# A row of exponentials per head, written to memory once per partition and read with shifted rows, in place of sixteen decay tiles, in a lightning-attention kernel

## The chip, the cores and the metric

The kernel runs on one core of a Trainium2 chip. The metric is the device time of one execution in microseconds (us); several executions are timed and the median counts. One more execution is taken with the hardware profiler, and every view of the profile comes from that one. Engines are named as in the profile: PE is TensorE's matmul, PEld its weight load, DVE is VectorE, ACT is ScalarE, POOL is GpSimd, SP is SyncE. SPq is SP's sequencer, which here issues nearly all DMAs.

## The reference, cut to what matters

The input x holds 4 sequences of 512 tokens with 512 features. It is normalised, goes through a linear attention with a decay per head, and is gated by a router.

```python
xn = layernorm(x)
qkv = silu(xn @ w_qkv.T)            # 16 heads of 128: q, k, v
# per head, slope s, blocks of BLK tokens, arr = 1 .. BLK
idx = arr[:, None] - arr[None, :]
diag_decay = where(idx >= 0, exp(-s * idx), 0)
o = (q * exp(-s * arr)) @ kv + ((q @ k.T) * diag_decay) @ v
kv = exp(-s * BLK) * kv + (k * exp(-s * (BLK - arr))).T @ v
o = norm_w * o * rsqrt(mean(o * o) + 1e-6) * sigmoid(xn @ w_gate.T)
s = o @ w_out.T
scores = softmax(xn @ router_w.T + router_b)      # 64 experts, the 8 largest count
g = silu(xn * sum(top8) + top8 @ expert_bias)
out = x + s * g
```

All is float32. The kernel uses blocks of 128 tokens in place of 64, which is the same sum cut elsewhere. What matters here is `diag_decay` with the decay of q: for one head both are made of the values exp(-s * d) for distances d from 0 to 128, and of zeros.

## The kernel before, in words

Every projection is a float32 product made of three passes over a hi and a lo part (`PASSES`): hi is a cast to the fast matmul type by ACT (`split_hi`, L100), lo is what is left, by DVE or POOL (`split_lo`, L103). A `unit` (matmuls at L496) computes a 2 x 2 block product with seven products in place of eight, from sums of blocks (S1 to S4 of the weights, T1 to T4 of the tokens); a `plain_unit` (L528) takes the eight products. The results of a unit are combined by DVE adds at L487, each of which reads the PSUM bank of a product.

The work runs in three stages. The **v stage** (0 to about 200 us) loads x in tiles of 128 tokens of two sequences, normalises them (`layer_norms`, `normalise_x` L204), transposes them on PE (`transpose`, pt at L253, copied to xf by ACT at L254), splits them into blocks (B11, T1, B21, B22 and the sums), computes the router's logits (lg, L314) and makes v in 16 units k = 0 to 15, eight for each half of the heads (`n1` is 8). The first two units are plain ones, while the sums of the weights are being made. `ws[0]` holds the weights of the first half, `ws[1]` those of the second. v goes to memory: the tiles `vo` come from a pool tagged `vout` with four buffers, one unit fills all four, and each is stored by a DMA at L582. The **head stage** (about 200 to 880 us) makes q, k and the gate per head and runs the attention. The **output stage** (880 us to the end) multiplies with w_out (po, L797).

The order of the work is written out by hand. A unit takes lists `after[0]` to `after[6]`, one for each of its products, with steps to be issued on all engines behind that product; the loop `for k, (p, t) in enumerate(tiles + again)` fills them. Each engine runs its own instructions in that order. DMAs of SP run on one queue in the order of issue, with eight completion semaphores taken in turn: a DMA waits for the one eight places before it. Four small loads at the start (slopes, rw, rb, nw, L878 to L881) are issued by ACT.

The decay tiles: `make_dist` writes two 128 x 128 tables of distances (POOL), `make_decays` takes 16 Exps of 128 x 256 on ACT (L168), `mask_decays` clears one triangle of each with an affine_select on POOL (L172) and stores each tile of 128 KB to memory (L177). In the head stage `load_decay` (L651) reads one tile per head and pair of sequences, 32 in all; the first 128 columns multiply the scores (`at`), the other 128 multiply q (`qd`). The Exps and selects run in three groups (7, 5 and 4 heads) among the first tile's work:

```python
make_decays(ds, hs[0])
prep[0]["stats"]()
prep[0]["norms"]()
ws[0].split_one("A11", nc.vector, hi=True)
prep[0]["turn"]()
load_pair(stage, *tiles[2])
mask_decays(ds, hs[0])
```

In the second half of the v stage, `load_xf` (L300) reads back xf of a tile (xf_again), from which POOL makes the blocks once more (`combine`); it is issued by SP in `after[0]` of the units k = 8 to 11.

Of the kernel before, what the change touches and what calls it, by code (L numbers as in the profile page):

```python
# [8 lines left out]
F32 = mybir.dt.float32  # L9
F32R = mybir.dt.float32r  # L10
AF = mybir.ActivationFunctionType
ALU = mybir.AluOpType
# [38 lines left out]
def kernel(  # L51
# [47 lines left out]
    def split_hi(hi, src):  # L99
        nc.scalar.copy(hi, src)  # L100
# [12 lines left out]
    dist = const.tile([P, 2, P], F32, tag="dist", name="dist")  # L113
    rest_of = const.tile([P, 1], F32, tag="rest_of", name="rest_of")
    kdecay = const.tile([P, NH], F32, tag="kdecay", name="kdecay")
    bdecay = const.tile([P, NH], F32, tag="bdecay", name="bdecay")

    decay_d = [dram.tile([P, 2, P], F32, tag=f"decay{h}", name=f"decay_{h}") for h in range(NH)]  # L120
    v_d = {
        (b, g): dram.tile([NT, P, VW], F32, tag=f"v{b}_{g}", name=f"v_{b}_{g}")
        for b in range(B) for g in range(NH // VH)
# [19 lines left out]
    def warm_up(n):  # L143
        ps = ps_o.tile([P, P], F32, tag="o", name="warm")
        for _ in range(n):
            nc.tensor.transpose(ps, ident, ident)

    def make_dist():  # L150
        nc.gpsimd.iota(
            dist[:, 0, :], pattern=[[-1, P]], base=0, channel_multiplier=1,
            allow_small_or_imprecise_dtypes=True,
        )
        nc.gpsimd.iota(
            dist[:, 1, :], pattern=[[-1, P]], base=-1, channel_multiplier=0,
            allow_small_or_imprecise_dtypes=True,
        )
# [4 lines left out]
        nc.gpsimd.tensor_scalar(dist[:, 0, :], dist[:, 0, :], 0.0, None, ALU.min)  # L163


    def make_decays(d, hs):
        for h in hs:
            nc.scalar.activation(d[h // 4][:, h % 4], dist, AF.Exp, scale=slopes[:, h : h + 1])  # L168

    def mask_decays(d, hs):  # L170
        for h in hs:
            nc.gpsimd.affine_select(  # L172
                d[h // 4][:, h % 4, 0], d[h // 4][:, h % 4, 0], pattern=[[1, P]],
                compare_op=ALU.is_ge, fill=0.0, base=0, channel_multiplier=-1,
            )
        for h in hs:
            nc.sync.dma_start(out=decay_d[h], in_=d[h // 4][:, h % 4])  # L177


    stats = [const.tile([P, NT, 2], F32, tag=f"stats{b}", name=f"stats{b}") for b in range(B)]  # L180
# [63 lines left out]
    xfs = {}  # L244


    def transpose(stage, p, j, t):
        b = p * PB + j
        if j == 0:
            xfs[p, t] = stage.tile([P, PB, FC, P], F32, tag="xf", name=f"xf_{p}_{t}", bufs=2)  # L250
        pt = ps_sc.tile([P, FC, P], F32, tag="sc", name=f"pt_{b}_{t}")
        for c in range(FC):
            nc.tensor.transpose(pt[:, c, :], xts[b, t][:, bass.ts(c, P)], ident)  # L253
        nc.scalar.copy(xfs[p, t][:, j], pt)  # L254

    def halves(xf):
        return xf[:, 0, 0:KC], xf[:, 1, 0:KC], xf[:, 0, KC:], xf[:, 1, KC:]
# [47 lines left out]
            nc.sync.dma_start(out=blocks_d[n][:, t], in_=blocks[p, n].bitcast(F32)[:, t])  # L305


    def logits(stage, p, t):
        if t == 0:
            scores[p] = stage.tile([P, PB, NT, E], F32, tag="scores", name=f"scores_{p}", bufs=2)  # L310
        ps = ps_sc.tile([P, PB, E], F32, tag="sc", name=f"lg_{p}_{t}")
        for j in range(PB):
            for c in range(FC):
                nc.tensor.matmul(  # L314
                    ps[:, j], xfs[p, t][:, j, c, :], rw[:, c, :], start=(c == 0), stop=(c == FC - 1)
                )
        nc.vector.tensor_tensor(
            scores[p][:, :, t, :], ps, rb[:, None, :].to_broadcast([P, PB, E]), ALU.add
        )
# [328 lines left out]

    def load_decay(p, h, attp):
        dec[p, h] = attp.tile([P, 2, P], F32, tag="dec", name=f"dec_{p}_{h}", bufs=3)  # L650
        nc.sync.dma_start(out=dec[p, h], in_=decay_d[h])  # L651


    def chunks(a):
# [198 lines left out]
    def load_pair(stage, p, t):  # L853
        for j in range(PB):
            load_x(stage, p * PB + j, t)
# [19 lines left out]
    make_first()  # L875

    nc.scalar.activation(kdecay[:, 0:NT], mhalf, AF.Exp)
    nc.scalar.dma_start(out=slopes, in_=slope.to_broadcast([P, NH]))  # L878
    nc.scalar.dma_start(out=rw, in_=router_w)
    nc.scalar.dma_start(out=rb, in_=router_b.to_broadcast([P, E]))  # L880
    nc.scalar.dma_start(out=nw, in_=norm_w)  # L881
    make_dist()
    warm_up(WARM)
# [5 lines left out]
    nc.scalar.activation(kdecay, slopes, AF.Exp, scale=rest_of[:, 0:1])  # L889
    nc.scalar.activation(bdecay, slopes, AF.Exp, scale=-float(P))  # L890
    ds = [
        sump.tile([P, KC * VW], F32, tag=f"sum{i}", name=f"mkdecay_{i}").rearrange(
            "p (h a m) -> p h a m", a=2, m=P
        ) for i in range(4)
    ]
    hs = range(0, 7), range(7, 12), range(12, NH)
    make_decays(ds, hs[0])
    prep[0]["stats"]()
    prep[0]["norms"]()
    ws[0].split_one("A11", nc.vector, hi=True)  # L900
    prep[0]["turn"]()
    load_pair(stage, *tiles[2])
    mask_decays(ds, hs[0])
    warm_up(6)
    prep[0]["sums"]()
    ws[0].split_one("A12", nc.gpsimd, 0)
    ws[0].split_one("A12", nc.vector, 1)
    prep[0]["logits"]()
    prep[1]["stats"]()
    ws[0].split_one("A21", nc.vector)  # L910
    make_decays(ds, hs[1])
    prep[1]["norms"]()
    load_pair(stage, *tiles[3])
    mask_decays(ds, hs[1])
    ws[0].split_one("A22", nc.gpsimd)
    make_decays(ds, hs[2])
    mask_decays(ds, hs[2])

    for k, (p, t) in enumerate(tiles + again):
        g, after = k // n1, nothing()  # L920
        for unit_of, what in ((n1 - 3, (0, "top")), (n1 - 2, (0, "less")), (n1 + 2, (1, "top")), (n1 + 3, (1, "less"))):
            if k == unit_of:
                after[2].append(lambda what=what: scores_less(*what))
        if n1 - NT <= k < n1:
            after[6].append(lambda p=p, t=t: keep_blocks(p, t))
        if k + 1 < n1:
            after[0 if k else 1].append(prep[k + 1]["turn"])
            if 0 < k < n1 - 3:
                after[0].append(lambda k=k: load_pair(stage, *tiles[k + 3]))
            after[1].append(prep[k + 1]["sums"])  # L930
            if k + 2 < n1:
                after[1].append(prep[k + 2]["stats"])
                after[4].append(prep[k + 2]["norms"])
            after[1].append(prep[k + 1]["plain"])
            after[4].append(prep[k + 1]["more"])
            after[4 if k else 6].append(prep[k + 1]["logits"])
        if k < NP_FIRST:
            for i in range(2 * k, 2 * k + 2):
                after[2 + 2 * (i % 2)].append(lambda i=i: ws[0].sum_of(i, nc.vector))
            for i, n in enumerate((("S1", "S2"), ("S3", "S4"))[k]):  # L940
                eng = nc.gpsimd if i else nc.vector
                after[2 * i + 3].append(lambda n=n, eng=eng: ws[0].split_one(n, eng))
        if k == NP_FIRST:
            after[0].append(ws[1].load())
# [12 lines left out]
        if n1 < k <= n1 + NT:  # L957
            sums, split_plain, split_sums = combine(stage, 0, k - n1 - 1, nc.gpsimd, "r")
            after[1] += [sums, split_plain]
            after[4].append(split_sums)  # L960
        if k == n1 + NT + 1:
            after[1].append(scores_exp)
        if k == 2 * n1 - 2:
            vs_stack.close()
            todo = [(p, *u) for p in range(NP) for u in h_units(p, hw_stack)]
            todo[0][3].load()()
            todo[1][3].load()()
        if k == 2 * n1 - 1:
            weight_steps(todo[0][3], after)
        v_unit(p, g, t, ws[g], vout, after, k < NP_FIRST)  # L970
# [184 lines left out]
```

## Time and profile before

| what | us |
|---|---|
| median of three executions | 1075.56 (1074.61 to 1075.66) |
| profiled execution | 1074.7 |
| its span, first to last instruction | 1073.0 |
| PE busy in it | 1058.8 |
| DVE, ACT, POOL busy | 686.3, 479.8, 724.2 |
| 16 Exps of the decay tiles, ACT, at | 5.50 to 20.5 in three groups |
| 16 selects, POOL, at | 7.85 to 22.5 in three groups |
| 16 stores of decay tiles, landed | 19.21 to 26.32 |
| first transpose, first logits, first v product | 7.51, 10.17, 11.98 |

The span leaves out what lies before the first and behind the last instruction, 1.7 us here. In a line of groups or of the timeline stand the start and the duration (or the busy sum), engine, line, operation, the tile written and the tile read, the sizes, and how often; brackets show the idle time before it and what ended it. In a list of waits stand what waited, what it waited for, the microseconds in total, how often, and the longest.

### The profile page before, as it was taken

The numbers are of one execution on the slowest core, as the hardware profiler recorded it, in microseconds if no ns is written. First come the engines' busy times: TensorE is split into PE (matmuls) and PEld (weight loads), VectorE is DVE, ScalarE is ACT, GpSimd is POOL, SyncE is SP. The second block draws the span as 40 slices with busy tenths as digits, with TensorE's granted clock in tenths as the row PEclk, the third lists the DMA queues.
The fourth block names the chain that finished last, engine by engine and source line by source line (L and its number), as shares of the span: only waits on it lengthen the run. The fifth ranks groups of instructions, "written<-read, shape, count | busy, mean of one in ns | idle before, by whom it ended". The sixth has DMA issues, their size and how long they took to land.

```text
span 1073.0 us, 16479 instructions
## 1 busy us (share of the span) xinstructions
PE 1058.8 (99%) x5762; PEld 909.6 (85%) x5762; DVE 686.3 (64%) x1059; ACT 479.8 (45%) x938; POOL 724.2 (67%) x725
## 2 busy tenths in 40 slices
PE   8999999999999999999999999999999999999998
PEld 7788788888888888888888888888888888788886
DVE  5898876667787565655755656556556565854554
ACT  7545545544444444444444444444444444331311
POOL 6898793867768677776786777767877757612130
PEclk9999999999999999999999999999999999999999
DMA  8556745422432223235722232233222428355351
GB/s 276 185 185 243 267 148 177 148 84 95 128 94 94 86 91 109 84 123 176 270 85 72 87 118 84 84 115 97 84 75 90 132 79 275 100 175 176 109 182 55
DMA packets 105059, 143.09 MB, mean 133 GB/s; under 512 B 9104, under 2 KB 53264, under 8 KB 104080
## 3 DMA queue, kind: packets, MB, share of 16 engines
q1 hardware_dynamic: 104112, 141.33, 39.9%
q8 instruction: 46, 0.75, 0.3%
q10 hardware_dynamic: 864, 0.70, 0.2%
q14 instruction: 37, 0.30, 0.1%
HBM read 91.14 MB, written 50.86 MB: 132 GB/s over the span
## 4 chain that ended last, share of the span: by engine, by line
PE 91%; DVE 5%; ACT 2%; DMA 1%; issue 1%; POOL 0%; SPq 0%; DVEq 0%; ACTq 0%; POOLq 0%
PE u_qk L496 27%; PE po L797 16%; PE u_g L496 14%; PE u_v L496 11%; PE sa L665 5%; PE o L702 5%; PE ss L688 4%; PE o L704 4%; PE kt L668 2%; DMA raw_v<-in_w_v_dram 1%; DVE vo_v L552 1%; PE lg L314 1%; PE pu L757 1%; DVE sum_v L432 1%; ACT w_A_v L100 0%
## 5 line engine op out<-in xcount | busy, mean ns | idle before, releaser
L797 PE MATMUL po<-wr,yr 128*128 128x512 f32 x768 | 180.0, 392 | 1.4 <-DVE u L791 1.4
L797 PEld LDWEIGHTS po<-wr,yr 128*128 128x128 f32 x768 | 144.8, 189 | 32.0 <-ACT yr L100 1.8
L496 PE MATMUL u_qk<-blk_T,ws_qk 128*128 128x512 f32 x576 | 149.1, 398 | 0.0
L714 POOL TENSOR_TENSOR sqs<-sqs,sq 128x512 f32<-128x512 f32 x60 | 77.2, 1287 | 90.3 <-ACT sq L713 86.7
L496 PEld LDWEIGHTS u_qk<-blk_T,ws_qk 128*128 128x128 f32 x576 | 104.7, 188 | 20.3
L692 DVE SCALAR_TENSOR_TENSOR st<-st,bdecay,ss 128x128 f32<-128x128 f32 x128 | 44.5, 348 | 105.2 <-ACT st L690 102.9
L496 PE MATMUL u_qk<-blk_B,wa_qk 128*128 128x512 f32 x384 | 99.6, 395 | 0.0
L103 DVE TENSOR_TENSOR yr<-yin,yr 128x512 fp32r<-128x512 f32 x64 | 68.7, 1109 | 46.5 <-ACT yr L100 46.5
L103 POOL TENSOR_TENSOR ws_qk<-sum_qk,ws_qk 128x512 fp32r<-128x512 f32 x64 | 88.4, 1392 | 14.7 <-ACT ws_qk L100 14.6
L702 PE MATMUL o<-at,vin 128*128 128x128 f32 x512 | 88.2, 274 | 0.0
L496 PEld LDWEIGHTS u_qk<-blk_B,wa_qk 128*128 128x128 f32 x384 | 70.8, 188 | 14.3
L702 PEld LDWEIGHTS o<-at,vin 128*128 128x128 f32 x512 | 77.2, 191 | 5.0
L496 PE MATMUL u_g<-blk_T,ws_g 128*128 128x512 f32 x288 | 77.8, 406 | 0.0
L674 ACT ACTIVATE kd<-kt,kdecay 128x384 f32<-128x384 f32 x64 | 37.3, 583 | 87.3 <-PE kt L668 87.3
L704 PE MATMUL o<-qd,st 128*128 128x128 f32 x384 | 74.2, 275 | 0.0
L665 PEld LDWEIGHTS sa<-q,k 128*128 128x128 f32 x512 | 66.6, 191 | 7.9 <-DVE q L552 2.7
L706 DVE SCALAR_TENSOR_TENSOR y<-o,nw,gt 128x512 f32<-128x512 f32 x64 | 47.9, 748 | 39.3 <-PE o L704 38.5
L549 ACT ACTIVATE sg_k<-k 128x512 f32<-128x512 f32 x64 | 40.5, 632 | 65.9 <-DVE k L487 65.9
L761 POOL TENSOR_TENSOR u<-u,sgu 128x512 f32<-128x512 f32 x16 | 20.7, 1292 | 72.6 <-ACT sgu L760 59.9
L665 PE MATMUL sa<-q,k 128*128 128x128 f32 x512 | 67.8, 275 | 1.7 <-DVE q L552 1.6
L676 POOL TENSOR_TENSOR qd<-q,dec 128x384 f32<-128x384 f32 x64 | 65.5, 1024 | 0.0
L496 PE MATMUL u_v<-w_S_v,blk_T 128*128 128x512 f32 x252 | 62.7, 392 | 1.3 <-DVE a_v L487 1.2
(182 smaller groups left out, 2424.3 us busy)
## 6 DMA issues: line engine op xcount, KB each, us to landing
v<-vo_v SPq DMA_DIRECT2D x64, 256.0 KB, 2.1
raw_qk<-in_w_head_dram SPq DMA_DIRECT2D x64, 256.0 KB, 4.0
vin<-v SPq DMA_DIRECT2D x64, 256.0 KB, 3.3
y<-y SPq DMA_DIRECT2D x64, 256.0 KB, 2.3
yin<-y SPq DMA_DIRECT2D x64, 256.0 KB, 3.9
x<-in_x_dram SPq DMA_DIRECT2D x32, 256.0 KB, 4.9
raw_g<-in_w_head_dram SPq DMA_DIRECT2D x32, 256.0 KB, 3.1
raw_v<-in_w_v_dram SPq DMA_DIRECT2D x16, 256.0 KB, 6.2
```

What stands on the lines that cost most here:

```text
L103: eng.tensor_tensor(lo, src, hi.bitcast(F32), ALU.subtract)
L496: nc.tensor.matmul(ps, lhsT, rhs, start=(first and c == 0 and n == 0), stop=(c == KC - 1 and n == len(PASSES) - 1), skip_group_check=not f ...
L549: nc.scalar.activation(sg, src, AF.Sigmoid)
L665: nc.tensor.matmul(pa[:, c], k[:, c], q[:, c], start=True, stop=True)
L676: nc.gpsimd.tensor_tensor(qd[s], q[:, 1:], d[:, 1, None, :].to_broadcast([P, NT - 1, P]), ALU.mult)
L688: nc.tensor.matmul(ps[:, c], kd[s][:, c], v_of(b, h, c), start=True, stop=True)
L692: nc.vector.scalar_tensor_tensor(r[:, c], r[:, c - 1], bdecay[:, h : h + 1], ps[:, c], ALU.mult, ALU.add)
L702: nc.tensor.matmul(o, v_of(b, h, c), at[s][:, c], start=True, stop=(c == 0))
L704: nc.tensor.matmul(o, st[s][:, c - 1], qd[s][:, c - 1], start=False, stop=True)
L706: nc.vector.scalar_tensor_tensor(y, po, nw[:, h : h + 1], gts[s], ALU.mult, ALU.mult)
L714: nc.gpsimd.tensor_tensor(sq[b], sq[b], s1, ALU.add)
L797: nc.tensor.matmul(pos[t], yr[:, yi, bass.ts(t, P)], wos[h][:, wi], start=(h == 0 and n == 0), stop=(h == NH - 1 and n == len(PASSES) - 1),)
```

## The change

There is one row of 256 values per head, in `decay_row`: 16 partitions, one per head. Column m holds exp(s * min(127 - m, 0)); columns 0 to 126 are then set to zero, so the row reads 0 (127 times), 1, exp(-s), exp(-2s) and so on to exp(-128s). A new small load brings one slope to each of the 16 partitions (`slope_of`).

`keep_decays` writes that row 128 times for each head into `decay_d` (16 x 128 x 256), as one DMA from the 16 partitions with a repeat. It is issued by SP in `after[2]` of unit k = 8. `load_decay` then makes two reads per tile: the first takes rows of 255 elements in place of 256, starting at element 127, so that each partition's row is shifted by one against the one before (this gives the triangle); the second takes columns 128 to 255 as they are.

The start is put in another order. The 16 Exps, 16 selects and 16 stores are gone; one Exp of 16 x 256 and a memset of 16 x 127 on POOL stand ahead of the first tile's statistics. A small Sigmoid ahead of them brings the load of ACT's function table forward. Of the first tile, DVE copies the transpose of the first sequence out of PSUM, ACT takes the hi part of B11 straight from PSUM, POOL its lo part, and ACT copies the transpose of the second sequence. The first logits are made in two halves, the second behind the first product step of unit 0. For tiles 2 and 3 the statistics and norms are issued earlier. In unit 8 the two pieces of the lo part of S4 are issued one step later each.

```diff
+    slope_of = const.tile([NH, 1], F32, tag="slope_of", name="slope_of")
+    decay_row = const.tile([NH, W], F32, tag="decay_row", name="decay_row")
-    decay_d = [dram.tile([P, 2, P], F32, tag=f"decay{h}", name=f"decay_{h}") for h in range(NH)]
+    decay_d = dram.tile([NH, P, W], F32, tag="decay", name="decay_d")
...
+    def make_decays():
+        nc.scalar.activation(decay_row, decay_row, AF.Exp, scale=slope_of)
+        nc.scalar.activation(kdecay, slopes, AF.Exp, scale=rest_of[:, 0:1])
+        nc.scalar.activation(bdecay, slopes, AF.Exp, scale=-float(P))
+        nc.gpsimd.memset(decay_row[:, 0 : P - 1], 0.0)
+
+    def keep_decays():
+        nc.sync.dma_start(out=decay_d, in_=decay_row[:, None, :].to_broadcast([NH, P, W]))
...
-        nc.sync.dma_start(out=dec[p, h], in_=decay_d[h])
+        rows = decay_d[h].rearrange("n m -> (n m)")[P - 1 : P - 1 + P * (W - 1)]
+        nc.sync.dma_start(
+            out=dec[p, h][:, 0], in_=rows.rearrange("(n m) -> n m", m=W - 1)[:, 0:P]
+        )
+        nc.sync.dma_start(out=dec[p, h][:, 1], in_=decay_d[h][:, P:W])
...
+    nc.scalar.dma_start(out=slope_of, in_=slope.rearrange("o h -> h o"))
...
-    make_decays(ds, hs[0])
+    make_decays()
+
+    nc.scalar.activation(sig, mhalf, AF.Sigmoid)
     prep[0]["stats"]()
     prep[0]["norms"]()
+
+    pt = [transpose(stage, 0, j, 0, False) for j in range(PB)]
+    nc.vector.tensor_copy(xfs[0, 0][:, 0], pt[0])
+    b11, b12, b21, b22 = halves(xfs[0, 0])
+    split_hi(blocks[0, "B11"][:, 0, 0], pt[0][:, 0:KC])
     ws[0].split_one("A11", nc.vector, hi=True)
-    prep[0]["turn"]()
+    split_lo(nc.gpsimd, blocks[0, "B11"][:, 0, 1], b11, blocks[0, "B11"][:, 0, 0])
+    nc.scalar.copy(xfs[0, 0][:, 1], pt[1])
+    nc.sync.dma_start(out=xf_d[0], in_=xfs[0, 0])
     load_pair(stage, *tiles[2])
-    mask_decays(ds, hs[0])
     warm_up(6)
-    prep[0]["sums"]()
+    split_blocks(0, 0, nc.vector, (("T1", b12), ("B21", b21), ("B22", b22)))
...
-    prep[0]["logits"]()
+    logits(stage, 0, 0, [0])
...
+            if k == 0:
+                after[1].insert(0, prep[2]["stats"])
...
-                after[4].append(prep[k + 2]["norms"])
+                after[4 if k > 1 else 3].append(prep[k + 2]["norms"])
...
+        if k == 0:
+            after[0].append(lambda: logits(stage, 0, 0, [1]))
...
-            ("S4", n1, 0, nc.vector, 0), ("S4", n1, 1, nc.vector, 1), ("A22", n1, 0, nc.gpsimd, None),
+            ("S4", n1, 1, nc.vector, 0), ("S4", n1, 2, nc.vector, 1), ("A22", n1, 0, nc.gpsimd, None),
...
+        if k == n1:
+            after[2].append(keep_decays)
```

More of the change, by code (lines that the diff above doesn't have):

```diff
@@ L112 @@
     mhalf = const.tile([P, NT], F32, tag="mhalf", name="mhalf")
-    dist = const.tile([P, 2, P], F32, tag="dist", name="dist")
+    W = 2 * P
+    slope_of = const.tile([NH, 1], F32, tag="slope_of", name="slope_of")
+    decay_row = const.tile([NH, W], F32, tag="decay_row", name="decay_row")
     rest_of = const.tile([P, 1], F32, tag="rest_of", name="rest_of")
@@ L151, in make_dist @@
         nc.gpsimd.iota(
[L152 to L156, printed above, removed]
+            decay_row, pattern=[[-1, W]], base=P - 1, channel_multiplier=0,
             allow_small_or_imprecise_dtypes=True,
@@ L162, in make_dist @@
         )
[L163 to L177, printed above, removed]
+        nc.gpsimd.tensor_scalar(decay_row, decay_row, 0.0, None, ALU.min)
+    def make_decays():
[5 more added lines that the diff above has]
+        nc.sync.dma_start(out=decay_d, in_=decay_row[:, None, :].to_broadcast([NH, P, W]))
     stats = [const.tile([P, NT, 2], F32, tag=f"stats{b}", name=f"stats{b}") for b in range(B)]
@@ L244, with transpose @@
     xfs = {}
-    def transpose(stage, p, j, t):
+    def transpose(stage, p, j, t, copy=True):
         b = p * PB + j
@@ L253, in transpose @@
             nc.tensor.transpose(pt[:, c, :], xts[b, t][:, bass.ts(c, P)], ident)
-        nc.scalar.copy(xfs[p, t][:, j], pt)
+        if copy:
+            nc.scalar.copy(xfs[p, t][:, j], pt)
+        return pt
     def halves(xf):
@@ L305, in keep_blocks, with logits @@
             nc.sync.dma_start(out=blocks_d[n][:, t], in_=blocks[p, n].bitcast(F32)[:, t])
-    def logits(stage, p, t):
-        if t == 0:
+    lg = {}
+    def logits(stage, p, t, js=range(PB)):
+        if t == 0 and 0 in js:
             scores[p] = stage.tile([P, PB, NT, E], F32, tag="scores", name=f"scores_{p}", bufs=2)
-        ps = ps_sc.tile([P, PB, E], F32, tag="sc", name=f"lg_{p}_{t}")
-        for j in range(PB):
+        if 0 in js:
+            lg[p, t] = ps_sc.tile([P, PB, E], F32, tag="sc", name=f"lg_{p}_{t}")
+        ps = lg[p, t]
+        for j in js:
             for c in range(FC):
@@ L316, in logits @@
                 )
+        if PB - 1 not in js:
+            return
         nc.vector.tensor_tensor(
@@ L882 @@
     make_dist()
+    sig = small.tile([P, NT], F32, tag="var", name="table")
     warm_up(WARM)
@@ L888 @@
         ws[0].place(n)
[L889 to L896, printed above, removed]
-    make_decays(ds, hs[0])
+    make_decays()
+    nc.scalar.activation(sig, mhalf, AF.Sigmoid)
     prep[0]["stats"]()
     prep[0]["norms"]()
+    pt = [transpose(stage, 0, j, 0, False) for j in range(PB)]
+    nc.vector.tensor_copy(xfs[0, 0][:, 0], pt[0])
+    b11, b12, b21, b22 = halves(xfs[0, 0])
+    split_hi(blocks[0, "B11"][:, 0, 0], pt[0][:, 0:KC])
     ws[0].split_one("A11", nc.vector, hi=True)
-    prep[0]["turn"]()
+    split_lo(nc.gpsimd, blocks[0, "B11"][:, 0, 1], b11, blocks[0, "B11"][:, 0, 0])
+    nc.scalar.copy(xfs[0, 0][:, 1], pt[1])
+    nc.sync.dma_start(out=xf_d[0], in_=xfs[0, 0])
     load_pair(stage, *tiles[2])
-    mask_decays(ds, hs[0])
     warm_up(6)
-    prep[0]["sums"]()
+    split_blocks(0, 0, nc.vector, (("T1", b12), ("B21", b21), ("B22", b22)))
     ws[0].split_one("A12", nc.gpsimd, 0)
     ws[0].split_one("A12", nc.vector, 1)
-    prep[0]["logits"]()
+    logits(stage, 0, 0, [0])
     prep[1]["stats"]()
     ws[0].split_one("A21", nc.vector)
-    make_decays(ds, hs[1])
     prep[1]["norms"]()
     load_pair(stage, *tiles[3])
-    mask_decays(ds, hs[1])
     ws[0].split_one("A22", nc.gpsimd)
-    make_decays(ds, hs[2])
-    mask_decays(ds, hs[2])
     for k, (p, t) in enumerate(tiles + again):
@@ L929 @@
                 after[0].append(lambda k=k: load_pair(stage, *tiles[k + 3]))
+            if k == 0:
+                after[1].insert(0, prep[2]["stats"])
             after[1].append(prep[k + 1]["sums"])
             if k + 2 < n1:
-                after[1].append(prep[k + 2]["stats"])
-                after[4].append(prep[k + 2]["norms"])
+                if k:
+                    after[1].append(prep[k + 2]["stats"])
+                after[4 if k > 1 else 3].append(prep[k + 2]["norms"])
             after[1].append(prep[k + 1]["plain"])
```

## The prediction

> **What bounds the kernel now.** First the page's busy table, the row of its slices and its chain.
>
> ```profile
> PE 1058.8 (99%) x5762; PEld 909.6 (85%) x5762; DVE 686.3 (64%) x1059; ACT 479.8 (45%) x938; POOL 724.2 (67%) x725
> ...
> PE   8999999999999999999999999999999999999998
> ...
> PE 91%; DVE 5%; ACT 2%; DMA 1%; issue 1%; POOL 0%; SPq 0%; DVEq 0%; ACTq 0%; POOLq 0%
> ```
>
> TensorE is busy for 1058.8 of 1073.0 us; DVE and ACT enter the chain in the first slice and at the late v stage. The change keeps every matmul, so it can win only where TensorE waits, 14.2 us in all, and lose wherever it makes TensorE wait. Next, PE's waits, longest sums first:
>
> ```profile
> PE pt L253 <- DVE x L204: 2.7, 5, 1.0
> PE sa L665 <- DVE q L552: 1.6, 2, 0.9
> PE po L797 <- DVE u L791: 1.4, 1, 1.4
> PE warm L146 <- POOL ident masks.py:199: 1.4, 1, 1.4
> PE u_v L496 <- DVE a_v L487: 1.2, 1, 1.2
> ```
>
> The edits reach the first row (transposes waiting for the normalised x) and the last; the others are elsewhere or are the start.
>
> **The start, 0 to 46 us.** Gone are 16 Exps on ACT (0.40 us apart, 6.4 us), 16 selects on POOL (0.40 apart, 6.4 us) and 16 stores of 128 KB on SP (0.34 us of the DMA line each). None of them is on PE; they delayed what is. The second sigmoid's table load (1.28 us at 20.52) moves ahead of the first tile, and the x norms of tiles 2 and 3 go ahead of the lo parts of S1 and S3, so the waits of the first row should shrink. From the A21 products at 18.80 to S2 at 45.36 PE takes 26.6 us for 24.3 us of matmuls (512 columns: six in 1.36 us): 2.3 us to win. Against it: the ACT queue's nw load now waits for the second x tile (landed 5.88) and stands ahead of the new Exp; Exp ends near 6.9, the POOL memset that waits for it near 7.1, and both rstd stand behind that memset on POOL. The first rstd was at 5.63 and the norm at 6.92; now about 7.2 and 7.8, so the first transpose moves from 7.51 to about 8.35. ACT takes blk_B11 straight from PSUM after DVE's copy (one bank), and A11 hi waits behind it on ACT; but only 8 of the 16 logits matmuls (2.00 us, 10.17 to 12.2) still stand before the first products, which pays the 0.85 us: they keep about their 11.98. A12 now waits for the landing of its lane's earlier load (6.97; it was issued at 5.90), A21 lands near 15 (14.81 before), and POOL's B11 lo stands before A12 lo: 1 to 2 us late at about 20 us. Together I take 0.3 us gained; bounds 1.5 gained, 1.0 lost.
>
> **S4 lo one step later.** In the first unit of the second half:
>
> ```profile
> 118.16 0.68 DVE L103 TENSOR_TENSOR w_S_v<-sum_v,w_S_v 128x512 fp32r<-128x512 f32 x1
> ...
> 118.76 0.68 DVE L487 TENSOR_TENSOR a_v<-u_v,s_v 128x512 f32<-128x512 f32 x1
> ...
> 119.49 0.74 PE L496 MATMUL u_v<-w_S_v,blk_T 128*128 128x512 f32 x2 [1.15 <-DVE a_v L487]
> ```
>
> The piece at 118.16 goes behind a_v, so a_v starts 0.6 earlier and PE waits 0.6 less. The second piece goes behind e_v; the S4 products at 121.26 still find it. 0.6 gained; bounds 0 and 1.1.
>
> **The decay reads.** 32 loads of 128 KB become 64 of 64 KB: 32 issues more at 0.33 to 0.54 us, 14 us of SP spread over 650. SP is idle there and each tile is asked for 15 us or more ahead, against landings of 3 to 6 us. Half of them read at a row step of 1020 bytes in place of 1024, in one more transfer; that lateness goes into the same 15 us. Nothing; without that cover 0.5 us per load, 16 us.
>
> **The decay write.** One DMA, 2048 rows of 1 KB = 2.10 MB, is put on SP behind the first xf_again and ahead of the four v stores of that unit.
>
> ```profile
> 121.77 0.60 SPq L300 DMA_DIRECT2D xf_again<-xfd  x1
> 122.52 5.76 SPq L582 DMA_DIRECT2D v<-vo_v  x4
> ```
>
> The queue behaves as one line in order of issue. The xf_again landed at 126.51 (its longest landing, 4.7 us), the four stores at 127.19, 127.81, 129.25 and 130.13. With a write of S us between, the stores land from 127.15 + S on, 0.65 apart. vout has four buffers, so unit 9's results reuse unit 8's:
>
> ```profile
> 131.10 0.69 DVE L487 TENSOR_TENSOR vo_v<-u_v,e_v 128x512 f32<-128x512 f32 x1 [1.77 <-PE u_v L496]
> ...
> 132.26 1.30 PE L496 MATMUL u_v<-w_A_v,blk_T 128*128 128x512 f32 x5
> ```
>
> The add at 131.10 overwrites the first store's source; the matmul at 132.26 writes the PSUM bank that the add reads and has 0.45 us to spare. The product behind the add waits for the third store, 1.3 after the first; it took 0.6 before, 0.7 more. So PE stalls S - 3.95 - 0.45 + 0.7 = S - 3.7 us. Queued behind the add on DVE is every later PSUM reader of the unit, so nothing goes round it. What is S? The old write of the same tiles:
>
> ```profile
> L177 SPq DMA_DIRECT2D decay<-mkdecay x16: 319/392/1178, 12.7 to 24.5; - x16
> ```
>
> Seven of these landed 0.33 to 0.39 us apart: 16 x 0.345 = 5.5 us, a stall of 1.8. But those came out of 128 partitions and the new one out of 16. The Trainium skill, "SBUF — State Buffer", section "Door 1: The DMA port swizzle", says that the rate follows how many of 16 ports the partitions reach: 16 partitions reach 4, 104 GB/s measured at 1 MiB, about 109 at most. That is 20.2 or 19.3 us: a stall of 16.5 or 15.6. The one row here with few partitions is the load into 64:
>
> ```profile
> L738 SPq DMA_DIRECT2D raw_eb<-in_expert_b_dram x1: 639/639/639, 894.2 to 894.2; - x1
> L739 SPq DMA_DIRECT2D raw_eb<-in_expert_b_dram x1: 589/589/589, 894.9 to 894.9; - x1
> ...
> DMA to landing us min/median/max: 6.6/6.8/7.0
> ```
>
> Issued at 894.20 and 894.88, they landed at 901.17 and 901.52, behind a woin that landed at 900.34: 1.18 us for 256 KB, 222 GB/s, where a 256 KB neighbour over all partitions took 0.61 to 0.69. Half the partitions, half the rate; a quarter should give 111 GB/s, S = 18.9. Row and page agree against the full-rate row, and I take S = 19.3: +15.6. The bounds are 1.8 and 16.5.
>
> **The clock behind the stall.** The trace shows one spell of a halved clock (start:end, length, busy us and count of PE, PEld, DVE, ACT, POOL, then granted clock, DMA share, GB/s):
>
> ```profile
> 895.00:896.00 1.00, 1.00 (x4) 0.80 (x3) 0.00 (x0) 0.17 (x1) 1.00 (x2) 0.54 0.97 291
> 896.00:897.00 1.00, 1.00 (x3) 0.74 (x3) 0.52 (x1) 0.63 (x2) 1.00 (x2) 0.50 0.97 363
> 897.00:898.00 1.00, 1.00 (x4) 0.78 (x3) 0.18 (x1) 0.93 (x2) 1.00 (x1) 0.50 1.07 410
> 898.00:899.00 1.00, 1.00 (x5) 0.82 (x4) 0.78 (x1) 0.75 (x2) 1.00 (x2) 0.75 1.10 291
> ```
>
> Lost: 0.46 + 0.50 + 0.50 + 0.25 = 1.7 us. The Trainium skill, "TensorE: Matmul & The Clock Gate", Part 1, says an idle window of about 3.4 us does that, so a 15.6 us stall buys it once: +1.7 (bounds 0 and 1.7); a 1.8 us stall would not.
>
> **Sum.** -0.3 - 0.6 + 15.6 + 1.7 = +16.4 on the span of 1073.0. The profiled execution took 1074.7 (1.7 outside the span), 0.86 below the median of 1075.56, so the median goes to 1092.0. The main case's bounds: -1.5 - 1.1 + 15.2 + 0 = +11.8 and +1.0 + 0 + 16.5 + 1.7 = +19.2; its likely range is 1088 to 1095.
>
> **Rivals.** The measurement tells 0.2% (2.15 us) from nothing. (1) Full rate: the line carries the write like the old stores, S = 5.5. For it: 16 heads can still be spread over the 16 DMA engines and the write goes to DRAM, while my partition row is a load. -0.3 - 0.6 + 1.8 = +0.9, 1076.5: not slower. It decides below S of about 6.7. Chance 0.17. (2) Hidden: the write or the stores go round each other, so only the gains stay: -0.9 to -2.6, 1073 to 1074.7. For it: other packets could be interleaved; against it the regular landings in order. 0.06. (3) In between: the port limit holds for part of it, S of 10 to 13, stall 6.3 to 9.3 with the clock: 1083 to 1086. 0.07. (4) Slower than the page: all engines read one partition's port at a time, S of several times 19; or the reads of 512 B come late. Above 1100, 0.03. The main case keeps 0.67.
>
> **How the numbers follow.** Forecast 1092.0. Range 1075.5 to 1097: it reaches from inside rival 1 over rival 3 to above the main case with the larger S and the start's loss (1.0 + 16.5 + 1.7 gives 1094.8), and leaves out (2), (4) and the lower third of (1), 0.15. Faster by over 0.2%: half of (2) and a little of (1), 0.05. Within: most of (1), half of (2), 0.17. Slower: 0.78.
>
> **What will show it.** After: PE idle of 15 us near 132 us, ended by DVE vo_v, itself released by the DMA v<-vo_v; a landing of the decay write about 23 us after issue; DMA GB/s near 109 at 127 to 146 us; granted clock 0.5 for 3 us behind it; a_v about 0.6 earlier; first transpose near 8.35, table load before 7. Wrong if the GB/s there is near 380, if stores land before the write, or if the v stage before 110 us moves by more than 1.5 us.

## The result, and the profile after

The changed kernel takes 1098.64 us (median of 4, 1097.42 to 1099.97), the kernel before on the same chip 1075.09 (1074.05 to 1075.66): 1.0224 times as long, interval 1.0212 to 1.0236. The forecast was 1092.0, in a range from 1075.5 to 1097. So the direction was right and the size was not: 23.5 us more in the medians where 16.4 was said. The profiled execution is the longest of the four, 1099.97 us with a span of 1098.1, 25.1 us above the span of before; the parts below add up to that span.

The page of the changed kernel:

```profile
PE 1068.1 (97%) x5762; PEld 912.9 (83%) x5762; DVE 684.9 (62%) x1059; ACT 475.0 (43%) x923; POOL 721.2 (66%) x710
...
PE   8999759999999999999999999999999999999998
...
PEclk9999979999999999999999999999999999999999
```

PE still has 5762 records, but it is busy for 9.3 us more, and at the same time idle for longer: the fifth and sixth slices are no longer full, and the sixth is the only one with a lowered clock. A hole was forecast there. That the same matmuls are also busy for longer was not; part of it is the lowered clock, the rest has another cause.

PE's waits in the changed kernel:

```profile
PE u_v L498 <- DVE vo_v L489: 18.8, 1, 18.8
PE pt L247 <- DVE x L198: 1.6, 2, 0.8
```

One wait of 18.8 us has appeared, at the add that the forecast named. The wait of before for a_v is gone, and the one for x has shrunk from 2.7 to 1.6. The tile of the decays, and the timeline around the wait:

```profile
L171 SPq DMA_DIRECT2D decay_d<-decay_row x1: 672/672/672, 119.9 to 119.9; - x1
...
DMA to landing us min/median/max: 2.6/3.3/27.5
```

```profile
148.10 0.69 DVE L489 TENSOR_TENSOR vo_v<-u_v,e_v 128x512 f32<-128x512 f32 x1 [20.80 <-DMA v<-vo_v]
...
148.85 2.50 PE L498 MATMUL u_v<-w_A_v,blk_T 128*128 128x512 f32 x5 [18.76 <-DVE vo_v L489]
```

The write was issued at 119.86 and landed 27.5 us later, at 147.34. The xf_again ahead of it landed at 124.48 and the first v store behind it at 147.98, so the write itself took 147.34 - 124.48 = 22.86 us for 2.10 MB: 92 GB/s. DVE's add waited for that store and PE for the add. The windows show the rate, and the clock (start:end, length, busy us and count of PE, PEld, DVE, ACT, POOL, granted clock, DMA share, GB/s):

```profile
126.00:128.00 2.00, 2.00 (x11) 1.65 (x10) 1.20 (x2) 0.74 (x2) 2.00 (x4) 1.00 0.83 94
...
132.00:134.00 2.00, 0.00 (x0) 0.00 (x0) 0.00 (x0) 0.00 (x0) 0.00 (x0) 0.78 0.83 93
...
148.00:150.00 2.00, 1.15 (x3) 0.96 (x4) 1.90 (x4) 1.11 (x3) 0.10 (x1) 0.50 0.54 215
150.00:152.00 2.00, 2.00 (x6) 1.52 (x5) 1.37 (x3) 1.27 (x4) 2.00 (x3) 0.50 0.39 152
152.00:154.00 2.00, 2.00 (x7) 1.61 (x6) 1.84 (x3) 0.63 (x1) 1.92 (x3) 0.60 0.36 138
```

The DMA engines call themselves 83% busy while they move 93 to 94 GB/s. PE went idle at 130.1; the trace's record of the clock shows half speed from 133.12 to 153.60, so PE, back at 148.85, worked at half speed for 4.75 us.

For the rest it helps to follow the start of the same matmul in both traces (they have equal numbers of records, in the same order but for the logits that the change moves in the first 20 us). The difference, after less before:

| place in the program | before, us | after less before |
|---|---|---|
| A21 products of tile 0 | 19.35 | +1.09 |
| unit 2 | 48.67 | -1.01 |
| end of first half of v | 117.72 | -1.15 |
| after the S4 products | 122.95 | -2.34 |
| first product after full clock is back | 135.21 | +18.91 |
| a late unit of the v stage | 187.57 | +18.91 |
| head stage, at one third | 414.75 | +20.66 |
| head stage, late | 876.57 | +23.73 |
| last matmul | 1067.94 | +24.98 |

Start -1.15, S4 -1.2, stall +18.8, slow clock +2.5 (21.25 in all from -2.34 to +18.91, less 18.76 of waiting), and then a creeping +6.1 between 190 us, where the products of the head stage begin, and the end, where the forecast has nothing. In the creeping part some of the 512-column matmuls start 4 to 11 ns later behind the one before than they did, most often 8, and the others as before. One group shows it: this is the line of the tile u_qk (ns min/median/max, first and last start), first of before and then of after.

```profile
L496 PE MATMUL u_qk<-blk_B,ws_qk x192: 387/389/486, 207.1 to 868.6; 128*128 128x512 f32 x192
```

```profile
L498 PE MATMUL u_qk<-blk_B,ws_qk x192: 393/396/481, 226.5 to 892.3; 128*128 128x512 f32 x192
```

The shortest went from 387 to 393 ns. The diff does not touch these matmuls. What it did touch is where their operands lie: `slope_of` is a new tile in the constant pool, takes 32 bytes there, and every tile allocated behind it on the left side of SBUF (blk, the v weights, four of the sixteen wr, part of yr) lies 32 bytes higher; the tiles of the right side (ws_qk, wa_qk, wb_qk, the rest of wr and yr) stay.

### The profile page after: what moved, and what is told of

The parts are those of the page before. It is cut to its first block, busy times and chain, and to the rows that moved or that the text cites. A ratio compares the mean times of both kernels' runs of the same rounds, so it can differ in the third digit from the quotient of the medians.

```text
span 1098.1 us, 16443 instructions
## 1 busy us (share of the span) xinstructions
PE 1068.1 (97%) x5762; PEld 912.9 (83%) x5762; DVE 684.9 (62%) x1059; ACT 475.0 (43%) x923; POOL 721.2 (66%) x710
## 4 chain that ended last, share of the span: by engine, by line
PE 92%; DMA 4%; DVE 2%; issue 1%; ACT 0%; POOL 0%; SPq 0%; DVEq 0%; ACTq 0%; POOLq 0%
PE u_qk L498 27%; PE po L803 16%; PE u_g L498 14%; PE u_v L498 12%; PE sa L671 5%; PE o L708 5%; PE ss L694 4%; PE o L710 4%; DMA v<-vo_v 2%; PE kt L674 2%; PE d_v L530 2%; DMA raw_v<-in_w_v_dram 1%; PE lg L314 1%; PE pu L763 1%; PE pt L247 1%
## 5 line engine op out<-in xcount | busy, mean ns | idle before, releaser
L103 POOL TENSOR_TENSOR ws_qk<-sum_qk,ws_qk 128x512 fp32r<-128x512 f32 x64 | 88.2, 1389 | 15.3 <-ACT ws_qk L100 15.2
L719 ACT ACTIVATE sq<-o 128x512 f32<-128x512 f32 x60 | 35.9, 598 | 63.2 <-DVE y L712 58.6
```

What stands on the lines that cost most here:

```text
L103: eng.tensor_tensor(lo, src, hi.bitcast(F32), ALU.subtract)
```

## The experiments

The short diffs are against the changed kernel, or against the kernel before where the name ends in "before".

### The creeping loss: placement, or something the stall leaves behind?

The edit of pad32_before:

```diff
-    ones = const.tile([P, 1], F32, tag="ones", name="ones")
+    ones9 = const.tile([P, 9], F32, tag="ones", name="ones")
+    ones = ones9[:, 0:1]
```

> The kernel before with one change: the small constant tile of ones is 9 elements wide in place of 1, so every tile of the left side behind it lies 32 bytes higher in SBUF, exactly as in the changed kernel, and nothing else differs. Theory (placement): the part of the loss that accrues after 206 us, about 6 us in small steps of 8 ns on the 512-column products, comes from this shift of 32 bytes between the tiles of the left and of the right side: 1079 to 1081 us. Rival (the creeping loss is what the 19 us stall or the other reads leave behind): 1075.1, no change.

Measured: 1080.54 us against 1074.76, ratio 1.0055 (1.0040 to 1.0070): +5.8. One line of padding in the kernel before brings the whole creeping loss; the group has the same 393 and 396 ns as in the changed kernel:

```profile
L497 PE MATMUL u_qk<-blk_B,ws_qk x192: 393/396/481, 207.0 to 872.8; 128*128 128x512 f32 x192
```

The edit of layout_after:

```diff
-    ones = const.tile([P, 1], F32, tag="ones", name="ones")
+    ones2 = const.tile([P, 2], F32, tag="ones", name="ones")
+    ones, slope_of = ones2[:, 0:1], ones2[0:NH, 1:2]
-    slope_of = const.tile([NH, 1], F32, tag="slope_of", name="slope_of")
```

> The changed kernel with the slope of each head kept in the free bytes behind the constant ones, so that all tiles lie where they lay before. The slow write stays. Theory (placement): the 6 us after 206 us are gone, the offset against before stays at the 18.9 us that it has after the stall: 1092.5. Rival (left behind by the stall): 1098.6.

Measured: 1092.66, ratio 1.0169 (1.0154 to 1.0185). The offset against before is 17.14 us at 165 us and 17.25 at 893: nothing creeps. The write took 21.6 us here (124.44 to 146.04) and PE waited 17.6. Placement is the cause, from both sides: added alone it costs 5.8, taken out alone it gives 6.0.

Which placement? In the trace of pad32_before each product's start-to-start time can be set against the same one of before, and sorted by the sides on which its two operands lie. By the addresses in the built program, which no trace shows, all of them agree modulo 256 bytes in the kernel before. In po of pad32_before: both on the left, 48 products, +0.06 ns each; both on the right, 558, +0.25; one on each side, 144, +6.33. In u_qk<-blk_B,ws_qk, always one on each side, +4.27; in the products of the v stage, both on the left, nothing. So not the new address hurts but the disagreement of the two operands. Three more runs with other distances:

The edit of pad256_before; pad64_before and pad128_before have 17 and 33 elements in place of 65:

```diff
-    ones = const.tile([P, 1], F32, tag="ones", name="ones")
+    ones_pad = const.tile([P, 65], F32, tag="ones", name="ones")
+    ones = ones_pad[:, 0:1]
```

> The kernel before with the ones 17 elements wide: all tiles of the left side lie 64 bytes higher. In the run with 32 bytes the slow products were those whose two operands lay at different places within 64 bytes (one at 0, the other at 32; 4 to 6 ns each), and not those with both at 0 or both at 32. Theory (relative place within 64 bytes): both are at 32 again, no loss: 1074.8. Rival (the move itself, whichever way it goes, costs, or the first placement was lucky in another way): about 1080 again.

> The kernel before with the tiles of the left side 128 bytes higher. A move by 32 bytes cost 5.8 us and one by 64 bytes 1.9, both on products whose two operands lie on different sides. Theory (the relative place within 128 bytes counts): no loss, 1075.0. Theory (it counts within 256 bytes, where all tiles of the kernel before agree): a loss that is left, 1076 to 1077. Rival (any move costs): 1077 or more.

> The same with 256 bytes: left and right tiles agree modulo 256 again. Both theories of relative place: 1075.0, and no slow products between the two sides. Rival (any move costs): 1077 or more.

The first of these expectations fell, and the second in part: with 128 bytes the loss is larger than either theory said and has the size that the rival named. What refutes the rival is the run with 256 bytes. 64 bytes: 1076.97 against 1075.02, ratio 1.0019 (1.0011 to 1.0027), +1.9. 128 bytes: 1079.81 against 1074.72, 1.0046 (1.0031 to 1.0061), +5.1. 256 bytes: 1074.78, 1.0000 (0.9991 to 1.0008), nothing. The same group with 64, 128 and 256 bytes:

```profile
L497 PE MATMUL u_qk<-blk_B,ws_qk x192: 388/394/482, 206.8 to 870.0; 128*128 128x512 f32 x192
```

```profile
L497 PE MATMUL u_qk<-blk_B,ws_qk x192: 387/395/478, 207.6 to 873.0; 128*128 128x512 f32 x192
```

```profile
L497 PE MATMUL u_qk<-blk_B,ws_qk x192: 387/389/486, 206.7 to 868.3; 128*128 128x512 f32 x192
```

Back to 389 ns only when left and right agree modulo 256 again. With 64 and with 128 bytes the mixed pairs of po are again the slow ones (+3.6 and +6.2 ns), those with both operands on the right are not (+0.1 to +0.3; the 48 with both on the left scatter by some 0.8 about nothing). What inside the chip makes a pair slow, and why 64 bytes cost a third of 32 and of 128, is open.

### The length of the write: partitions, or rows and bytes?

The edit of rep128_after:

```diff
-    decay_row = const.tile([NH, W], F32, tag="decay_row", name="decay_row")
+    decay_row = const.tile([P, W], F32, tag="decay_row", name="decay_row")
-    nc.scalar.dma_start(out=slope_of, in_=slope.rearrange("o h -> h o"))
+    nc.scalar.dma_start(out=slope_of, in_=slope.rearrange("o h -> h o").to_broadcast([NH, P // NH]))
-        nc.sync.dma_start(out=decay_d, in_=decay_row[:, None, :].to_broadcast([NH, P, W]))
+        rows = decay_d.rearrange("h (r n) m -> (h r) n m", n=NH)
+        nc.sync.dma_start(out=rows, in_=decay_row[:, None, :].to_broadcast([P, NH, W]))
```

> The changed kernel with the row of each head held by 8 partitions in place of one (128 partitions in all), each written 16 times: same place on the queue, same bytes, same rows of 1 KB in memory, same placement of tiles as in the changed kernel. Theory (partitions): the write takes 5.5 us in place of 22.9, the stall is 1 to 2 us in place of 18.8, the clock stays full: 1079 us with the creeping loss, 1073.5 if that loss was left behind by the stall. Rival (the length is due to 2048 rows or to the bytes, not to the partitions): 1098.6.

Measured: 1081.94, ratio 1.0071 (1.0056 to 1.0086). The tile of the decays and PE's wait:

```profile
L172 SPq DMA_DIRECT2D decay_d<-decay_row x1: 633/633/633, 121.2 to 121.2; - x1
...
DMA to landing us min/median/max: 2.5/3.3/9.9
```

```profile
PE u_v L499 <- DVE vo_v L490: 1.2, 1, 1.2
```

From the landing ahead of it (125.68) to its own (131.07) are 5.39 us, 389 GB/s: the same bytes in the same 2048 rows of 1 KB, from 128 partitions. This edit also reads each row 16 times in place of 128, but that is not the cause: the pieces of split8_layout, below, read each row 16 times as well, from 16 partitions, and a piece with hardly anything beside it moved 102 GB/s:

```profile
157.60:160.20 2.60, 2.60 (x14) 2.13 (x13) 0.57 (x2) 0.60 (x1) 2.60 (x4) 1.00 0.79 102
```

The stall is 1.2 us and no clock is lost. The forecast's rule, write less 3.7, gives 1.7 here, 17.9 in layout_after (17.6 measured) and 19.2 in the changed kernel (18.8 measured). The median is 2.9 above the 1079 expected, and 1.3 of it is seen in the trace: the load of 128 single slopes, four bytes each, lands at 4.14 and is followed by later landings, of the second x tile (from 4.78 to 5.46), of rw (from 7.13 to 8.16) and of the third part of the v weights, A21, whose cast moves from 15.12 to 16.44; the first half of v begins 1.3 us later than in the changed kernel. The rest of the 2.9 is open.

### Does another issuing engine let the stores pass?

The edit of actq_after:

```diff
-        nc.sync.dma_start(out=decay_d, in_=decay_row[:, None, :].to_broadcast([NH, P, W]))
+        nc.scalar.dma_start(out=decay_d, in_=decay_row[:, None, :].to_broadcast([NH, P, W]))
```

> The changed kernel with the write issued by ACT in place of SP, at the same step. Theory (one line per issuing queue): the stores of v no longer stand behind the write but take turns with it; a store still meets slow packets, so I expect a stall of 0 to 8 us in place of 18.8: 1079 to 1088. Rival (all DMAs of the core stand in one line, whichever engine issues them): 1098.6.

Measured: 1102.58, ratio 1.0261 (1.0244 to 1.0278), worse than the changed kernel. PE's waits and the write:

```profile
PE u_v L498 <- ACT s_v L504: 12.4, 1, 12.4
PE u_v L498 <- DVE vo_v L489: 7.8, 1, 7.8
```

```profile
L171 ACTq DMA_DIRECT2D decay_d<-decay_row x1: 663/663/663, 113.2 to 113.2; - x1
...
DMA to landing us min/median/max: 2.5/3.2/28.9
```

The write is issued at 113.22 in place of 119.86, since ACT comes to it earlier than SP, and lands at 142.13. SP's stores do not take useful turns with it: a block store that SP issued at 118.01 landed at 137.90, and in the window 118 to 120 the whole core moved 93 GB/s, the pace of the write alone. The stall is cut in two (20.2 together), not shortened, and behind each part the clock is halved, which takes another 4.1 us in the offsets. So the expected 0 to 8 us was wrong and the rival nearer: by the rate, what SP issued had to keep the pace of the slow reads, though it stood in another queue.

### Is it the buffers of v?

The edit of vout7_layout, beside the placement of layout_after:

```diff
-    vwp, vout = left(vw_stack, "vw", 8), left(vw_stack, "vout", 4)
+    vwp, vout = left(vw_stack, "vw", 8), left(vw_stack, "vout", 7)
```

> The changed kernel with the old placement of tiles and seven buffers for the results of v in place of four; the slow write in one piece as it was. Theory (TensorE stalls because a result needs a buffer whose store stands behind the write): three more results can be made first, about 1.4 us apart, so the stall shrinks from 17.6 by about 4 us: 1088.5. Rival (TensorE waits for something else that stands behind the write, such as xf_again): 1092.7.

Measured: 1088.36, ratio 1.0133 (1.0113 to 1.0153).

```profile
PE u_v L498 <- ACT s_v L504: 13.5, 1, 13.5
```

17.6 became 13.5. Three more buffers buy 4.1 us, as said for three more results; the releaser is now ACT's copy of the next unit, which stands behind the result that found no buffer. The chain is what the forecast said: store behind write, buffer behind store, PSUM reader behind buffer, PE behind reader.

### S4 alone

The edit of s4_before:

```diff
-            ("S4", n1, 0, nc.vector, 0), ("S4", n1, 1, nc.vector, 1),
+            ("S4", n1, 1, nc.vector, 0), ("S4", n1, 2, nc.vector, 1),
```

> The kernel before with nothing but the two pieces of the lo part of S4 issued one step later each. Theory: the TensorE wait of 1.15 us for a_v goes and 0.25 us comes back at the fourth last product, as in the changed kernel: 1073.7 to 1074.0. Rival (the wait moves to the S4 products instead): 1074.8 or more.

Measured: 1074.39 against 1075.02, ratio 0.9994 (0.9986 to 1.0003): not told from no change, and short of what was expected. PE's wait went from 1.2 to

```profile
PE u_v L496 <- DVE a_v L487: 0.6, 1, 0.6
```

which is the 0.6 less that the forecast named, and in the offsets it gains 0.4 us. In every version with the changed start the same edit gains 1.1 to 1.2 (-1.15 to -2.34 in the table). So about 0.8 us of it belongs to the two edits together. DVE has more lead with the changed start: it begins a_v 0.87 us before PE wants the product behind it (116.15 and 117.02 in the changed kernel), in s4_before only 0.18 before PE would have been ready (117.88 and 118.06). Where that lead comes from is open.

### A version that beats both

First the write in pieces, still out of 16 partitions:

The edit of split8_layout, beside the placement of layout_after:

```diff
-    def keep_decays():
-        nc.sync.dma_start(out=decay_d, in_=decay_row[:, None, :].to_broadcast([NH, P, W]))
+    def keep_decays(i):
+        nc.sync.dma_start(
+            out=decay_d[:, bass.ts(i, NH)], in_=decay_row[:, None, :].to_broadcast([NH, NH, W])
+        )
-        if k == n1:
-            after[2].append(keep_decays)
+        if k >= n1:
+            after[2].append(lambda k=k: keep_decays(k - n1))
```

> The changed kernel with the old placement of tiles and the same slow write from 16 partitions, cut into eight writes of 16 rows per head, one in each of the units 8 to 15. Each should take a little under 3 us, which the stores can be late by without TensorE waiting (the stall was the write's length less 3.7). Theory: no stall, no halved clock, only the gains of the start and of S4 stay: 1092.7 - 17.6 - 1.8 = 1073.3, faster than before by 1 to 2 us. Rival (each piece brings its own stall or its own fixed cost of 2 us in line): 1076 to 1082.

Measured: 1074.38, ratio 0.9992 (0.9984 to 1.0001), from 1072.23 to 1076.71. Seven of the eight pieces can be told apart by their packets: they took 1.6 to 2.7 us from the first packet to the last. PE has no u_v wait left in its list and the clock stays full behind the writes, so the stall is gone; but the gain is smaller than expected. The profiled execution is the slowest of twelve. In it the first half of v began 1.5 us later than before, where the changed kernel began 1.15 earlier, with the same code, and 1.6 us more went at the change of stages near 895 us, where the clock was halved for 6.83 us in place of 3.41. Its timeline at the norms of tile 1:

```profile
17.25 2.68 POOL L103 TENSOR_TENSOR w_A_v<-raw_v,w_A_v 128x512 fp32r<-128x512 f32 x2
17.32 2.89 DVE L200 TENSOR_SCALAR x<-x,stats,rstd 128x512 f32<-128x512 f32 x2
...
18.95 0.63 PE L249 MATMUL pt<-ident,x 128*128 128x128 f32 x4 [1.13 <-DVE x L200]
...
20.36 1.09 PE L249 MATMUL pt<-ident,x 128*128 128x128 f32 x4 [0.78 <-DVE x L200]
```

Two norms took 2.89 us beside POOL's lo part of A22, which started only at 18.97 in the kernel before. In the changed kernel POOL began between the two, and the second alone was slow:

```profile
17.41 1.96 DVE L198 TENSOR_SCALAR x<-x,stats,rstd 128x512 f32<-128x512 f32 x2
17.63 2.88 POOL L103 TENSOR_TENSOR w_A_v<-raw_v,w_A_v 128x512 fp32r<-128x512 f32 x2 [1.28 <-ACT w_A_v L100]
```

Over all traces a norm takes 0.54 or 0.55 us, and 1.48 to 1.50 where POOL's subtraction had begun before it; POOL came first only in split8_layout and vout7_layout, by 0.07 us. In these two PE then had little to do, and the clock was halved for 3.41 us, here from 20.31:

```profile
18.00:20.00 2.00, 0.63 (x4) 0.42 (x4) 2.00 (x2) 0.84 (x2) 1.93 (x2) 1.00 0.00 0
20.00:22.00 2.00, 1.64 (x6) 1.57 (x7) 1.93 (x7) 0.72 (x3) 0.00 (x0) 0.58 0.54 139
```

Hence the edit of a22_split8 against split8_layout:

```diff
-    ws[0].split_one("A22", nc.gpsimd)
+    ws[0].split_one("A22", nc.vector)
```

> The changed kernel with the old placement of tiles, the write cut into eight, and the lo part of A22 made by DVE behind the norms of tile 1 in place of by POOL. With POOL at it from 17.3 us, the two norms of tile 1 took about 1 us and more each in place of 0.55 and the transposes of tile 1 came apart (18.95 and 20.36). Theory: those transposes close up, 1.4 us less: 1073.0 against 1074.4 of the version with POOL. Rival (the products of A22 come late instead, since DVE starts the lo part only behind the norms): 1074.4 or more.

Measured: 1072.62 against 1074.72, ratio 0.9981 (0.9974 to 0.9988).

```profile
17.27 1.00 DVE L200 TENSOR_SCALAR x<-x,stats,rstd 128x512 f32<-128x512 f32 x2
...
17.97 1.08 PE L249 MATMUL pt<-ident,x 128*128 128x128 f32 x8 [0.20 <-DVE x L200]
```

The norms take 1.00 us together, the eight transposes run on end, the clock stays full there, and the products of A22 do not wait. In the medians this is 1.8 us less than split8_layout; the means, each against its own kernel before, differ by 1.1 (0.2 to 2.0). This version is faster than the changed kernel by 26 us (1098.64 - 1072.62) and than the kernel before by 2.1.

And nw_a22_split8 against a22_split8:

```diff
-    nc.scalar.dma_start(out=nw, in_=norm_w)
     make_dist()
...
     nc.scalar.activation(sig, mhalf, AF.Sigmoid)
+    nc.scalar.dma_start(out=nw, in_=norm_w)
```

> The same, and the nw load, which waits on ACT for the landing of the second x tile and stands ahead of the Exp of the decay row, is issued behind that Exp and the table load. Theory: Exp, memset and both rstd start about 1 us earlier, and A12 is issued without waiting for an earlier weight load; the first products wait for A11 anyway, so 0 to 0.7 us less than without it: 1072.3 to 1073.0.

Measured: 1072.74, ratio 0.9982 (0.9974 to 0.9991): no difference from the version without it. The first products do wait for A11 and not for the norm.

## Why the prediction was wrong

The sum had four terms, and the decay reads at nothing. With what the profiled execution shows:

| term | forecast | measured |
|---|---|---|
| start | -0.3 | -1.15 |
| S4 one step later | -0.6 | -1.2 |
| stall behind the write | +15.6 | +18.8 |
| halved clock behind it | +1.7 | +2.5 |
| placement of tiles | none | +6.1 |
| sum | +16.4 | +25.0 |

- **The missing term.** The step that failed is the first of the working: "The change keeps every matmul, so it can win only where TensorE waits, 14.2 us in all, and lose wherever it makes TensorE wait." That leaves the pace of the matmuls themselves out of the sum, without a reason. A new tile of four bytes moved the operands of one side by 32 bytes, and the mixed pairs became slower without any wait: +6.1 in the trace, +5.8 for the shift alone (pad32_before), 6.0 back without it (layout_after). Nothing in the profile of before could show it; the allocation of the two programs could. Without this term the median is 1092.66 (layout_after), inside the range and 0.7 from the forecast, though 17.9 above its own kernel before where 16.4 was said.
- **That closeness is partly luck.** In layout_after stall and clock cost 2.3 more than said, and start and S4 gave 1.5 more than said. The mechanism of the stall was right at each link (rep128_after, vout7_layout), and the rule "write less 3.7" held within 0.5 us at three lengths. The length was mis-sized: S = 19.3 was taken from a row of 64 partitions and from the page of the Trainium skill, "SBUF — State Buffer", section "Door 1: The DMA port swizzle", which gives 104 GB/s measured and about 109 at most for 16 partitions. The runs show 92 and 97 (22.86 and 21.60 us). The measurement decides: 3.2 us more stall in the changed kernel. With a write of 19.3 us the median would by this have been near 1095.4 (1098.6 less 3.2, an estimate), just inside the range; so the miss of the range took both, and placement is the larger.
- **Two slips in the working.** "Half the partitions, half the rate; a quarter should give 111 GB/s" counts the page's ports: 16 of 128 partitions are an eighth, and by partitions the same row gives 55 GB/s. The row is weak besides, since its two loads go to different halves of the partitions and landed 0.83 and 0.35 us behind what stood before them. And the lower bound of the sum, -1.5 - 1.1 + 15.2, is +12.6 and not +11.8; the range from 1088 follows from 12.6.
- **The full-rate rival** was refuted for 16 partitions and confirmed for 128: had the write come from 128, its 5.5 us and a stall below 2 would have been right.
- **The clock.** One spell at half speed, as said, but outside its bounds of 0 to 1.7: it cost 2.5, since PE worked at half speed for 4.75 us, where the row of before had 3.41. In each trace these spells lie on a grid of 3.41 us: apart from the last, which the end of the run cuts off, they last 3.41, 6.83, 13.65, 17.07 or 20.48. So the cost differs with where PE's return falls in the grid: over five returns from a stall in four runs PE stayed at half speed for 3.0 to 6.0 us.
- **The start** lay inside its bounds, but not by the steps named. The first transpose came at 7.57 and not at 8.35, and the first products at 9.91 and not at their old 11.98: the first x landed at 3.49 in place of 4.42, the second at 4.78 in place of 5.88, and the forecast left the landings where they were. In all eight traces with a load of single slopes put ahead of the four small loads the first x landed by 3.64, in the six without it at 4.39 or later; no run changes that load alone.
- **A21's products** came 1.09 late, as said, but by luck: A21 landed at 15.05, near the 15 of the forecast, and what was late were the transposes ahead, behind the second norm of tile 1, slow beside POOL. With A22 off POOL (a22_split8) the same products come at their old time. Of the 2.3 us named between A21 and S2, 2.0 were won.
- **The gain of the start is not steady.** Of the other versions with A22 on POOL, layout_after and actq_after began unit 2 earlier than before (1.19 and 1.43), rep128_after 0.30 later, and vout7_layout and split8_layout, with both norms slow and the clock halved, 1.10 and 1.49 later.
- **S4.** The mechanism was right, since alone it shortens the wait by the 0.6 named (s4_before). The size was not: alone it gains 0.4 in the trace, with the changed start 1.2.
- **The decay reads** cost nothing, as said: without the shift of placement the offset moves by 0.11 us from 210 to 893 us (layout_after), with all 64 reads in it.

## What to carry to other kernels

A change can cost by its allocation alone: compare the addresses of the operands of the bounding engine before and after. Here it paid to keep the two operands of a 512-column matmul equal modulo 256 bytes, by putting the new small tile into free bytes. Before a large DMA is called hidden, ask how many partitions it reads and what stands behind it in line; cut it into pieces shorter than the slack of the store behind (here 1.6 to 2.7 us against 3.7). Another queue did not help here. And when work is taken off an engine, look at what that engine does next at the same time, and which neighbour it slows.

## What was not expected of the hardware

- Two operands of a 512-column matmul that lie differently modulo 256 bytes: about 2 to 6 ns more per matmul on average at 32 bytes, and 5.8 us per run at 32 bytes, 1.9 at 64, 5.1 at 128, 0 at 256.
- A DMA that reads 16 partitions keeps a second queue's transfers back as well: 93 GB/s for the whole core while both had work.
- Two DVE norms of 128x512 took 1.00 us without POOL at work and 2.89 beside POOL subtractions of the same size. What decides is which begins first: POOL first by 0.07 us slowed both norms, DVE first by 0.11 us (actq_after) left the first at full pace.
- The halved clock at the change of stages near 895 us, which the forecast used as its row, comes and goes with the same instructions there: 3.41 us in before, 6.83 in split8_layout, none in five of the fourteen traces. Where it was missing (a22_split8) PE was 1.6 us further ahead of before at 900 us and had lost that again by 930, in part to three waits for wr (1.2 us). So the 1.7 us that the row shows are lost on the spot, and in that comparison not in the whole run.
